# Eight-bit edge counts, four strips and counts dealt evenly to the steps, in a three-layer graph network on one core

## The chip, the core and the metric

The kernel runs on one core of one Trainium2 chip. The metric is device time in microseconds (us). The core has a matrix engine (TensorE, PE in the profile; its weight loads are PEld), a vector engine (VectorE, DVE), an activation engine (ScalarE, ACT), a general engine (GpSimd, POOL) and a queue engine (SyncE, SP). ACT, POOL and SP also issue transfers between DRAM and on-chip memory. Each engine works through its own instructions in program order.

## What is computed

A graph has N = 6250 nodes with 256 features and E = 200000 edges, sorted by their end node `dst`. End nodes follow a square law, so low nodes have by far the most edges: node 0 alone has some 2500, the last ones about 16. Start nodes `src` are random. Three graph convolutions come first, then a mixture-of-depths feed-forward layer:

```python
h = relu(gcn(layernorm(x), W1, b1)); h = relu(gcn(h, W2, b2)); x = x + gcn(h, W3, b3)
# gcn(h): msg = (h @ W)[src] * norm; segment_sum(msg, dst) + b
#         with one self-loop per node, norm = dinv[src] * dinv[dst]
weights = layernorm(x) @ wr + br          # the 3124 nodes of highest weight are chosen
y = (gelu(sel @ w1 + b1) @ w2 + b2) * w_sel
out = x_in_place_of_not_chosen + y_scattered_to_chosen   # residual on the layernormed x, added to x
```

## The kernel before

Nodes are cut into 49 tiles of 128. The first 31 tiles of end nodes (`DENSE`) are summed by **counts**: a matrix that holds, for each pair (start node, end node), how many edges join them. The sum over edges is then a matrix product of counts and node features. The other 18 tiles are summed by **gathers**: rows of start nodes are fetched by index, 128 edges at a time (a chunk; 359 chunks in 180 sets of two), and added to their end nodes with a one-hot matrix.

*One tile by counts.* A strip `[128, 49, 128]` in 16-bit floats holds a tile's counts for all 49 tiles of start nodes. It is used in seven pieces of seven start tiles. Each piece is one **step**: `piece_of` (L725) casts it to 32 bits, on ACT (L728) or, where `CASTS` says so, on VectorE (L730); `add_up` (L733) then does seven matmuls of 128x512 into the sum `c_pa` (L736). 512 columns are the features as a rounded part and a rest. `prepare` casts two steps ahead (`AHEAD`).

*Making counts (layer 0 only).* A window is 2, 3 or 4 neighbouring end nodes, with a fixed number of 128-edge slots, from an estimate of its edges. `one_hot` (L661, VectorE, L669) makes two one-hot tensors for K = 12 slots, `hot_w` for (start tile, end node in the window) and `hot_l` for the start node in its tile; each has two buffers. One count matmul (L689) per slot multiplies them into a window's place in a PSUM bank `ps_b` (two buffers). Windows fill a bank in threes (width 3), fives (width 2) or twos. `count_bank` (L678) makes a whole bank and evicts it to the strip on ACT (L705). `counted` (L714) checks the largest count of the one tile that could pass the exact range, adds the self-loops on VectorE (L722) and writes the strip to the DRAM tensor `counts` (L723), for layers 1 and 2.

*The order in layer 0.* All four compute engines follow an order written by hand. Tiles run from 30 down to 0, so the fullest comes last. Tile 30 is counted ahead of the loop. While a tile is summed, the next tile's banks are made, as planned in the table `place` (L830 to 834): the next tile's banks are divided evenly, by number of banks, over steps 0 to 4 of the seven, and between two banks comes a share of the step's seven sum matmuls (L902 to 906). There are two strips, used in turn. Count matmuls per step vary with the slots that windows have; for tile 0 they are 107, 71, 40, 46 and 42, for a tile of width 3 they are 9, 9, 9, 9 and 7.

*Gathers and the rest.* In each step a share of the sets is fetched by indirect transfers (L600, GpSimd), one-hot matrices are made (L609, VectorE), and in layers 1 and 2 the rows are split into two parts (L619 ACT, L624 VectorE). The matmuls are L632, with L637 for the self-loops. A finished tile goes through `total` (L527, L528), transposes (L287), the product with the next weights (L298) and a store (L545). Twenty columns of edge ends are fetched, coded and transposed into a `ps_b` bank (L795, `flip`) during the first layer.

*Layers 1 and 2* load each piece of counts from DRAM (`load`, L931: tile `whole`), cast it and sum as above. In layer 2, VectorE also does the residual and the norm (L549 to L576). The choice of nodes and the feed-forward layer follow.

Of the kernel before, what the change touches and what calls it, by code (L numbers as in the profile page):

```python
# [9 lines left out]
FP = mybir.dt.float32  # L10
FR = mybir.dt.float32r
F16 = mybir.dt.float16
BF = mybir.dt.bfloat16
I32 = mybir.dt.int32
U16 = mybir.dt.uint16
AF = mybir.ActivationFunctionType
AX = mybir.AxisListType
OP = mybir.AluOpType
# [3 lines left out]
P = 128  # L22
# [6 lines left out]
NT = (N + P - 1) // P  # L29
# [15 lines left out]


NOWHERE = 1 << 20
EXACT = 2048
RC = 200
RN = E // RC  # L50
K = 12
WMAX = 4
PIECE = 7
DENSE = 31
GB = 2
MSGS = [4, 7, 7]
LATE = [12, 6]
CASTS = [(0, 4), (0, 3), (3,)]
BANK = 512
# [7 lines left out]
def windows():  # L67

    banks = []
    for t in range(DENSE):  # L70
        n = P
# [16 lines left out]
BANKS = windows()  # L88
TILES_BY = list(range(DENSE))[::-1]

SOURCES = [(3, 2, 4, 1, 5, 6, 0), (0, 1, 2, 3, 5, 4, 6)]
SLOTS = [(a, w, c) for t in TILES_BY for bank in BANKS[t] for a, w, n in bank for c in range(n)]
WIDTH = [w for _, w, _ in SLOTS]
MOST = [max(n for bank in t for _, _, n in bank) for t in BANKS]
SD = ceil(len(SLOTS) / P)

CHUNKS = [(t, k, n) for t in range(DENSE, NT) for n in [chunks_of(t * P, t * P + P)] for k in range(n)]
# [10 lines left out]
def by_counts(  # L108
# [29 lines left out]


    rows = dram.tile([NP, 2 * D + 1], FP, name="c_rows")  # L140
    counts = dram.tile([DENSE, P, NT * P], F16, name="counts")

    sent = [dram.tile([NP, 2 * D if i == 0 else D], FR if i == 0 else FP, name=f"sent{i}") for i in range(3)]
    ends = {}
# [4 lines left out]
    b1p = build.enter_context(tc.tile_pool(name="b1p", bufs=1))  # L149
# [3 lines left out]
    f3p = hots.enter_context(tc.tile_pool(name="f3p", bufs=2))  # L153
# [57 lines left out]
    ident = keep.tile([P, P], FP, name="c_ident")  # L211
# [17 lines left out]
    ident_h = keep.tile([P, P], F16, name="c_ident_h")  # L229
    nc.vector.tensor_copy(ident_h, ident)  # L230
# [77 lines left out]
    for i, n in ((0, P), (1, NT)):  # L308
        made = f1p.tile([HP, HC, n], BF, name=f"hot_h{i}")
# [175 lines left out]
    later = {}  # L485
# [171 lines left out]
    ps_b = hots.enter_context(tc.tile_pool(name="ps_b", bufs=2, space=PSUM))  # L657
    later["g"] = hots.enter_context(tc.tile_pool(name="ps_g1", bufs=2, space=PSUM))
    hot = {}

    def one_hot(s):  # L661

        n = min(K, SD * P - s)
        assert {s // P, (s + n - 1) // P} <= columns_made
        wide = NT * max(WIDTH[s : s + K])
        made = []
        for up, cols, code, name in ((up_w, wide, codes[:, 0, s : s + n], "hot_w"), (up_l, P, codes[:, 1, s : s + n], "hot_l")):
            rows_k = b2p.tile([P, K // 2, up.shape[1], 2], F16, name=name)
            nc.vector.tensor_tensor(  # L669
                rows_k[:, : n // 2, :cols, :],  # L670
                up[:, None, :cols, :].to_broadcast([P, n // 2, cols, 2]),
                code.rearrange("p (k two) -> p k two", two=2)[:, :, None, :].to_broadcast([P, n // 2, cols, 2]),
                op=OP.is_equal,
            )
            made.append(rows_k)
        return made

    def count_bank(strip, t, bank, s):  # L678
        pb = ps_b.tile([P, BANK], FP, name="ps_b")
        at_c = 0  # L680
        for node, width, chunks in bank:
            for c in range(chunks):
                k = s % K
                if k == 0:
                    hot[s] = hot.pop(s, None) or one_hot(s)
                if k == K // 4 and s - k + K < len(WIDTH):
                    hot[s - k + K] = one_hot(s - k + K)
                row_w, row_l = hot[s - k]
                nc.tensor.matmul(  # L689
                    pb[:, at_c : at_c + NT * width],  # L690
                    row_l[:, k // 2, :, k % 2], row_w[:, k // 2, : NT * width, k % 2],
                    start=(c == 0), stop=(c == chunks - 1),
                )
                s += 1
                if k == K - 1:
                    hot.pop(s - K)
            at_c += NT * width

        at_c = 0
        i = 0  # L700
        while i < len(bank):
            node, width, _ = bank[i]
            n = sum(1 for w in bank[i:] if w[1] == width)
            d0 = node - t * P
            nc.scalar.activation(  # L705
                strip[:, :, d0 : d0 + n * width].rearrange("p h (a j) -> p h a j", j=width),
                pb[:, at_c : at_c + n * NT * width].rearrange("p (a h j) -> p h a j", a=n, j=width),
                AF.Copy,
            )
            at_c += n * NT * width  # L710
            i += n
        return s

    def counted(strip, t):  # L714
        if MOST[t] * P >= EXACT:
            top = small.tile([P, 1], FP, name="top")
            large = max(a - t * P + w for bank in BANKS[t] for a, w, n in bank if n * P >= EXACT)
            nc.vector.tensor_reduce(top, strip[:, :, :large], axis=AX.XY, op=OP.max)
            nc.vector.tensor_scalar(top, top, float(EXACT), None, op0=OP.is_ge)
            nc.vector.tensor_add(bad[:, 1:2], bad[:, 1:2], top)  # L720

        nc.vector.tensor_add(strip[:, t, :], strip[:, t, :], ident_h)  # L722
        nc.sync.dma_start(counts[t], strip.rearrange("p h d -> p (h d)"))  # L723

    def piece_of(layer, counts_7, i):  # L725
        piece = later["l3"].tile([P, PIECE, P], FR, name="piece")
# [17 lines left out]
    NS = NT // PIECE  # L744
    AHEAD = 2
# [79 lines left out]
    strips = {}  # L825
    pieces = {}
    s = 0
    order = [(t, i) for t in TILES_BY for i in range(NS)]

    place = {}  # L830
    for t, u in zip(TILES_BY, TILES_BY[1:]):
        m = len(BANKS[u])
        for i in range(NS - AHEAD):
            place[t, i] = BANKS[u][m * i // (NS - AHEAD) : m * (i + 1) // (NS - AHEAD)]

    now["due"] = pace(len(order) - 2 * NS, LATE[0]) + [SETS] * 2 * NS

# [26 lines left out]
    first_tile = TILES_BY[0]  # L864
# [2 lines left out]
    flip()  # L867
    next_step()
    send_x(1)
    strips[first_tile] = f3p.tile([P, NT, P], F16, name="strip", bufs=1)  # L870
# [13 lines left out]
    by_turn = [f3p, later["2"]]  # L884
    load_b(0, later["2"], nc.sync)
    load_w(1, later["2"], nc.sync)
    for n in range(AHEAD):
# [1 line left out]
    for n, (t, i) in enumerate(order):  # L889
        prepare(0, now, n, order, cast)  # L890

        flip()
        if taken and (taken[0][0] >= SD or (taken[0][0] - 2) * P <= s):
            next_column()
        if i == 0:
            pa = new_sums()
            u = TILES_BY[n // NS + 1] if n + NS < len(order) else None
            if u is not None:
                strips[u] = by_turn[(n // NS + 1) % 2].tile([P, NT, P], F16, name="strip", bufs=1)

        banks = place.get((t, i), [])
        m = max(1, len(banks))  # L902
        for k in range(m):
            if banks:
                s = count_bank(strips[u], u, banks[k], s)
            add_up(pa, pieces[n], i, range(PIECE * k // m, PIECE * (k + 1) // m))
        gathered(0, now, now["due"][n])
        if banks and i == NS - AHEAD - 1:
            counted(strips[u], u)
        pieces.pop(n)  # L910
        if i == NS - 1:
            onward(0, t, pa)
            strips.pop(t)
        next_step()
    finish()
    guard.close()
    firsts.close()
# [5 lines left out]
    l8p = lay.enter_context(tc.tile_pool(name="l8p", bufs=8))  # L923
# [5 lines left out]
    nc.sync.dma_start(wr_sb, wr.rearrange("d o -> o d").to_broadcast([P, D]))  # L929

    def load(t, i):  # L931
        whole = l8p.tile([P, PIECE, P], F16, name="whole")
        nc.sync.dma_start(
            whole.rearrange("p h d -> p (h d)"), counts[t][:, i * PIECE * P : (i + 1) * PIECE * P]
        )
        return whole

    with tc.manual_schedule(engines=ordered):
        for layer in (1, 2):
# [4 lines left out]
            order = [(t, i) for i in sources for t in range(2)]  # L944
# [74 lines left out]
    for i, (shift, n) in enumerate(DIGITS):  # L1019
# [7 lines left out]
            op=OP.is_ge,  # L1027
# [37 lines left out]
    place = places(kept, "place")  # L1065
# [14 lines left out]
    hot = ffn.tile([P, TC, NT], BF, name="hot")  # L1080
# [5 lines left out]
    for a in range(0, NT, PIECE):  # L1086
# [5 lines left out]
            op=OP.is_equal,  # L1092
        )
        for j in range(PIECE):
            t = a + j
# [19 lines left out]
    for g, n in enumerate(groups):  # L1115
        a = sum(groups[:g])
# [586 lines left out]
```

## Time and profile before

| What | Value |
|---|---|
| median of three runs | 2147.77 us (2144.26 to 2150.42) |
| profiled execution, its own time | 2141.61 us |
| its span, first to last instruction | 2139.8 us |
| busy PE / PEld | 1903.7 us (89%) / 1456.1 us (68%) |
| busy DVE / ACT / POOL | 1360.4 (64%) / 1162.1 (54%) / 1268.1 us (59%) |
| layer 0, first sum matmul to last tile's start | 144.0 to 847.0 us |
| count matmuls L689 | 2171, of them 1269 of 98 columns, 806 of 147, 96 of 196 |
| evictions L705 | 441, 247.8 us busy on ACT |
| loads `whole`<-`counts` | 434 of 224.0 KB |
| stores `counts`<-`strip` | 31 of 1568.0 KB |

The span leaves out 1.8 us around the first and the last instruction. A line of the page such as the two below names source line, engine, operation, what is written and read, the shape and the number, then busy us, mean ns of one, and the idle time of the engine ahead of them with what ended it. Here TensorE's largest group and its count matmuls:

```profile
L736 PE MATMUL c_pa<-hl,piece 128*128 128x512 f32 x4557 | 1257.5, 408 | 22.9 <-DVE hl L953 14.1
L689 PE MATMUL ps_b<-hot_w,hot_l 128*128 128x98 f16 (+2 forms) x2171 | 211.5, 224 | 60.5 <-DVE hot_l L669 49.5
```

Ends of matmuls are modelled and overlap their neighbours (408 ns is more than the distance between two), so distances between starts tell more than lengths do.

### The profile page before, as it was taken

How to read it: one execution, taken by the hardware profiler on the slowest of the kernel's cores; microseconds unless marked ns; L12 is line 12 of the kernel's file. 1: busy time of each engine (PE TensorE's matmuls, PEld its weight loads, DVE VectorE, ACT ScalarE, POOL GpSimd, SP SyncE). 2: the span in 40 equal slices, each digit the busy share in tenths (PEclk: the TensorE clock that was granted, in tenths of full speed). 3: DMA queues.
4: the chain of work that ended last, by engine and by line, in shares of the span. 5: the costliest groups of instructions: out<-in, count | busy, mean ns of one | idle time of the engine just before them, and what ended most of it. 6: DMA issues, size and time to landing. Idle time of an engine off the chain costs nothing.

```text
span 2139.8 us, 30448 instructions
## 1 busy us (share of the span) xinstructions
PE 1903.7 (89%) x9636; PEld 1456.1 (68%) x9636; DVE 1360.4 (64%) x3370; ACT 1162.1 (54%) x1986; POOL 1268.1 (59%) x1228
## 2 busy tenths in 40 slices
PE   4949999999999887799999999889999999928997
PEld 3726767777766666488888888667777777715665
DVE  7686565667677777555555555488888888862111
ACT  3676666656655533656555555576666665502111
POOL 5425777667766520477777777377777777602221
PEclk9969999999999999899999999999999999958999
DMA  8387888898977640877777777598888888612210
GB/s 211 93 295 227 248 256 267 246 269 231 274 217 205 197 145 36 290 235 224 215 215 210 215 213 214 170 285 261 255 256 255 255 255 251 205 58 62 60 48 17
DMA packets 229052, 435.60 MB, mean 204 GB/s; under 512 B 35358, under 2 KB 139092, under 8 KB 224881
## 3 DMA queue, kind: packets, MB, share of 16 engines
q0 software_dynamic: 92992, 205.70, 35.2%
q1 hardware_dynamic: 104357, 192.11, 28.0%
q10 hardware_dynamic: 31532, 35.75, 4.9%
q8 instruction: 78, 1.28, 0.2%
q14 instruction: 93, 0.76, 0.1%
HBM read 335.50 MB, written 99.61 MB: 203 GB/s over the span
## 4 chain that ended last, share of the span: by engine, by line
PE 60%; DVE 21%; DMA 8%; issue 4%; ACT 3%; POOL 3%; ACTq 0%; SPq 0%; POOLq 0%; DVEq 0%
PE c_pa L736 32%; PE ps_g L632 8%; PE c_po L1144 4%; PE c_ph L1136 4%; PE ps_b L689 4%; PE c_pt L298 4%; DVE hot_w L669 3%; DVE hot_l L669 3%; DVE half L624 2%; DMA msg<-sent,source 2%; DMA c_xt<-in_x 2%; DMA half<-sent,source 2%; POOL msg L600 2%; DVE pick_sel L609 1%; DVE c_z L528 1%
## 5 line engine op out<-in xcount | busy, mean ns | idle before, releaser
L736 PE MATMUL c_pa<-hl,piece 128*128 128x512 f32 x4557 | 1257.5, 408 | 22.9 <-DVE hl L953 14.1
L736 PEld LDWEIGHTS c_pa<-hl,piece 128*128 128x128 f32 x4557 | 828.1, 190 | 189.7 <-DVE hl L953 15.8
L600 POOL DMA_INDIRECT msg<-sent,source x718 | 733.3, 1021 | 346.6 <-issue 145.0
L600 POOL DMA_INDIRECT half<-sent,source x359 | 389.9, 1086 | 200.1 <-issue 75.6
L609 DVE TENSOR_TENSOR pick_sel<-up_h,local 128x256 fp32r<-128x256 f16 x540 | 227.8, 422 | 281.6 <-PE ps_g L632 280.4
L632 PE MATMUL ps_g<-half,pick_sel 128*128 128x512 f32 x1077 | 347.7, 401 | 40.1 <-DVE half L624 32.7
L619 ACT ACTIVATE half<-msg 128x512 fp32r<-128x512 f32 x360 | 225.4, 626 | 233.8 <-PE ps_g L632 157.3
L728 ACT ACTIVATE piece<-whole 128x896 fp32r<-128x896 f16 x341 | 320.2, 942 | 57.2 <-PE c_pa L736 31.2
L705 ACT ACTIVATE strip<-ps_b 128x441 f16<-128x441 f32 (+3 forms) x441 | 247.8, 570 | 175.5 <-PE ps_b L689 165.9
L624 DVE TENSOR_TENSOR half<-msg,half 128x512 fp32r<-128x512 f32 x360 | 248.7, 691 | 82.0 <-ACT half L619 80.4
L632 PEld LDWEIGHTS ps_g<-half,pick_sel 128*128 128x128 f32 x1077 | 200.2, 189 | 100.1 <-DVE half L624 49.0
L689 PE MATMUL ps_b<-hot_w,hot_l 128*128 128x98 f16 (+2 forms) x2171 | 211.5, 224 | 60.5 <-DVE hot_l L669 49.5
L689 PEld LDWEIGHTS <-hot_l 128*128 128x128 f16 x2171 | 133.4, 100 | 174.7 <-issue 104.0
L728 ACT ACTIVATE piece<-strip 128x896 fp32r<-128x896 f16 x159 | 151.2, 952 | 99.5 <-PE c_pa L736 94.3
L669 DVE TENSOR_TENSOR hot_w<-up_w,codes 128x1176 f16<-128x1176 f16 (+2 forms) x181 | 165.7, 915 | 41.8 <-PE ps_b L689 41.6
L669 DVE TENSOR_TENSOR hot_l<-up_l,codes 128x1536 f16<-128x1536 f16 x181 | 172.5, 953 | 0.0
L1140 ACT ACTIVATE ht<-c_ph,b_sb 128x512 f32<-128x512 f32 (+2 forms) x64 | 38.0, 594 | 186.4 <-PE c_ph L1136 186.2
L1152 POOL DMA_INDIRECT out<-o,pick x25 | 25.2, 1007 | 138.4 <-DVE o L1149 138.4
L1148 DVE TENSOR_TENSOR o<-c_po,b_sb 128x256 f32<-128x256 f32 x25 | 10.6, 425 | 149.2 <-PE c_po L1144 149.2
L298 PE MATMUL c_pt<-c_wg,c_zt 128*128 128x256 f32 x392 | 99.9, 380 | 0.5 <-ACT c_zt L293 0.5
L1136 PE MATMUL c_ph<-yt,w_sb 128*128 128x512 f32 (+2 forms) x256 | 89.4, 506 | 0.6 <-DVE yt L1131 0.6
L1144 PE MATMUL c_po<-w_sb,ht 128*128 128x256 f32 x400 | 88.0, 379 | 0.0
(218 smaller groups left out, 1532.0 us busy)
## 6 DMA issues: line engine op xcount, KB each, us to landing
whole<-counts SPq DMA_DIRECT2D x434, 224.0 KB
counts<-strip SPq DMA_DIRECT2D x31, 1568.0 KB
c_rows<-ys ACTq DMA_DIRECT2D x49, 256.5 KB
sent<-hl SPq DMA_DIRECT2D x7, 1792.0 KB
sent<-c_h ACTq DMA_DIRECT2D x98, 128.0 KB
message<-sent SPq DMA_DIRECT2D x98, 128.0 KB
msg<-sent,source POOLq DMA_INDIRECT x718
c_xt<-in_x SPq DMA_DIRECT2D x48, 128.0 KB
```

The source lines that it names most:

```text
L298: nc.tensor.matmul(pt[:, 1, :], zt[:, k, :], w_sb[:, k, :], start=(k == 0), stop=(k == KD - 1))
L600: nc.gpsimd.indirect_dma_start(out=out_j, out_offset=None, in_=sent[layer], in_offset=bass.IndirectOffsetOnAxis(ap=source[:, i : i + 1], a ...
L609: nc.vector.tensor_tensor(pick[:, :n], up_h[:, None, :].to_broadcast([P, n, P]), local[:, b * GB : b * GB + n, None].to_broadcast([P, n, P ...
L619: nc.scalar.activation(half[:, :n, 0, :], msg[:, :n], AF.Copy)
L624: nc.vector.tensor_sub(half[:, :n, 1, :], msg[:, :n], half[:, :n, 0, :].bitcast(FP))
L632: nc.tensor.matmul(open_sums[t], pick[:, j, :], half[:, j].rearrange("p two d -> p (two d)"), start=(k == 0), stop=False)
L669: nc.vector.tensor_tensor(rows_k[:, : n // 2, :cols, :], up[:, None, :cols, :].to_broadcast([P, n // 2, cols, 2]), code.rearrange("p (k tw ...
L689: nc.tensor.matmul(pb[:, at_c : at_c + NT * width], row_l[:, k // 2, :, k % 2], row_w[:, k // 2, : NT * width, k % 2], start=(c == 0), sto ...
L705: nc.scalar.activation(strip[:, :, d0 : d0 + n * width].rearrange("p h (a j) -> p h a j", j=width), pb[:, at_c : at_c + n * NT * width].re ...
L728: nc.scalar.activation(piece, counts_7, AF.Copy)
L736: nc.tensor.matmul(pa, piece[:, j, :], hl[:, q].rearrange("p two d -> p (two d)"), start=(i == sources[0] and j == 0), stop=(i == sources[ ...
L1136: nc.tensor.matmul(ph[:, : n * P], w1_sb[:, k, f * P : (f + 1) * P], yt[:, k, : n * P], start=(k == 0), stop=(k == KD - 1),)
```

## The change

1. Counts are held in eight-bit unsigned integers: the strips, the DRAM tensor `counts`, the identity that adds self-loops, and the loaded pieces `whole`.
2. An eviction whose windows have more than one slot (105 of the 441) also gives the sum of what it writes, per partition, into a column of `row_sums`. A new `all_counted` takes the largest of these sums once, at the end of layer 0, and flags a value of 255 or more. The check by tile in `counted` goes.
3. There are four strips in place of two, with half the bytes each, so the same memory. A tile's counts may be begun up to three tiles ahead.
4. `count_bank` is split into `count_window` and `evict`. The unit of the plan is a window, no longer a bank. A window costs its slots times (128 + columns); the plan goes through all steps and hands out windows at the lowest steady rate that meets every tile's deadline, two steps ahead of its first use. Within a step, single windows alternate with shares of the seven sum matmuls. A bank can stay open from one step to the next.

By this plan the count matmuls per step are 9 or 10 in the first four tiles (all seven steps), for instance 13, 13, 11, 0, 0, 14, 13 in the middle, and 18, 15, 18, 16, 18, 16, 16 in the 27th tile.

```diff
-EXACT = 2048
+EXACT = 255
+STRIPS = 4
-    counts = dram.tile([DENSE, P, NT * P], F16, name="counts")
+    counts = dram.tile([DENSE, P, NT * P], U8, name="counts")
-    def count_bank(strip, t, bank, s):
-        pb = ps_b.tile([P, BANK], FP, name="ps_b")
...
+    def count_bank(strip, t, bank, s):
+        for j in range(len(bank)):
+            s = count_window(bank, j, s)
+        evict(strip, t, bank)
+        return s
+    in_making = []
+    def count_window(bank, j, s):
+        if j == 0:
+            in_making.append(ps_b.tile([P, BANK], FP, name="ps_b"))
+        pb = in_making[0]
+        at_c = sum(NT * w for _, w, _ in bank[:j])
+        _, width, chunks = bank[j]
+        for c in range(chunks):
...
+    def evict(strip, t, bank):
+        pb = in_making.pop()
...
+            held = None
+            if max(w[2] for w in bank[i : i + n]) * P >= EXACT:
+                held = row_sums[:, len(summed_up) : len(summed_up) + 1]
+                summed_up.append(node)
             nc.scalar.activation(
...
                 AF.Copy,
+                accum_out=held,
             )
     def counted(strip, t):
-        if MOST[t] * P >= EXACT:
...
-        nc.vector.tensor_add(strip[:, t, :], strip[:, t, :], ident_h)
+        nc.vector.tensor_add(strip[:, t, :], strip[:, t, :], ident_8)
         nc.sync.dma_start(counts[t], strip.rearrange("p h d -> p (h d)"))
+    def all_counted():
+        top = small.tile([P, 1], FP, name="top")
+        nc.vector.tensor_reduce(top, row_sums[:, : len(summed_up)], axis=AX.X, op=OP.max)
+        nc.vector.tensor_scalar(bad[:, 1:2], top, float(EXACT), None, op0=OP.is_ge)
-    place = {}
-    for t, u in zip(TILES_BY, TILES_BY[1:]):
-        m = len(BANKS[u])
-        for i in range(NS - AHEAD):
-            place[t, i] = BANKS[u][m * i // (NS - AHEAD) : m * (i + 1) // (NS - AHEAD)]
+    todo = []
+    for k, u in enumerate(TILES_BY[1:], 1):
+        for bank in BANKS[u]:
+            for i, (_, w, c) in enumerate(bank):
+                todo.append((max(0, (k - STRIPS + 1) * NS - AHEAD), k * NS - AHEAD - 1, c * (P + NT * w), u, bank, i))
+    place = [[] for _ in order]
+    credit = 0
+    for n in range(len(order)):
+        rate = 0
+        ahead = -credit
+        for _, until, work_of, _, _, _ in todo:
+            ahead += work_of
+            rate = max(rate, ahead / (until - n + 1))
+        credit += rate
+        while todo and todo[0][0] <= n and todo[0][2] / 2 <= credit:
+            credit -= todo[0][2]
+            place[n].append(todo.pop(0)[3:])
+        credit = min(credit, todo[0][2] / 2) if todo else 0
-        banks = place.get((t, i), [])
-        m = max(1, len(banks))
+        made = place[n]
+        m = max(1, len(made))
         for k in range(m):
-            if banks:
-                s = count_bank(strips[u], u, banks[k], s)
+            if made:
+                u, bank, j = made[k]
+                if bank is BANKS[u][0] and j == 0:
+                    strips[u] = new_strip(u)
+                s = count_window(bank, j, s)
+                if j == len(bank) - 1:
+                    evict(strips[u], u, bank)
+                    if bank is BANKS[u][-1]:
+                        counted(strips[u], u)
             add_up(pa, pieces[n], i, range(PIECE * k // m, PIECE * (k + 1) // m))
-        whole = l8p.tile([P, PIECE, P], F16, name="whole")
+        whole = l8p.tile([P, PIECE, P], U8, name="whole")
```

More of the change, by code (lines that the diff above doesn't have):

```diff
@@ L15 @@
 U16 = mybir.dt.uint16
+U8 = mybir.dt.uint8
 AF = mybir.ActivationFunctionType
@@ L93 @@
 WIDTH = [w for _, w, _ in SLOTS]
-MOST = [max(n for bank in t for _, _, n in bank) for t in BANKS]
 SD = ceil(len(SLOTS) / P)
@@ L228, in by_counts @@
     nc.vector.tensor_scalar(last, diff_i, float(1 - P), None, op0=OP.is_equal)
-    ident_h = keep.tile([P, P], F16, name="c_ident_h")
-    nc.vector.tensor_copy(ident_h, ident)
+    ident_8 = keep.tile([P, P], U8, name="c_ident_8")
+    nc.vector.tensor_copy(ident_8, ident)
     ident_r = keep.tile([P, P], FR, name="c_ident_r")
@@ L678, in count_bank @@
     def count_bank(strip, t, bank, s):
-        pb = ps_b.tile([P, BANK], FP, name="ps_b")
[L680 to L697, printed above, removed]
+        for j in range(len(bank)):
[10 more added lines that the diff above has]
+        for c in range(chunks):
+            k = s % K
+            if k == 0:
+                hot[s] = hot.pop(s, None) or one_hot(s)
+            if k == K // 4 and s - k + K < len(WIDTH):
+                hot[s - k + K] = one_hot(s - k + K)
+            row_w, row_l = hot[s - k]
+            nc.tensor.matmul(
+                pb[:, at_c : at_c + NT * width],
+                row_l[:, k // 2, :, k % 2], row_w[:, k // 2, : NT * width, k % 2],
+                start=(c == 0), stop=(c == chunks - 1),
+            )
+            s += 1
+            if k == K - 1:
+                hot.pop(s - K)
+        return s
+    def evict(strip, t, bank):
+        pb = in_making.pop()
         at_c = 0
@@ L711, in count_bank @@
             i += n
-        return s
+    row_sums = b1p.tile([P, sum(len(t) + 1 for t in BANKS if max(w[2] for bank in t for w in bank) > 1)], FP, name="row_sums")
+    summed_up = []
     def counted(strip, t):
-        if MOST[t] * P >= EXACT:
[L716 to L722, printed above, removed]
+        nc.vector.tensor_add(strip[:, t, :], strip[:, t, :], ident_8)
         nc.sync.dma_start(counts[t], strip.rearrange("p h d -> p (h d)"))
+    def all_counted():
+        top = small.tile([P, 1], FP, name="top")
+        nc.vector.tensor_reduce(top, row_sums[:, : len(summed_up)], axis=AX.X, op=OP.max)
+        nc.vector.tensor_scalar(bad[:, 1:2], top, float(EXACT), None, op0=OP.is_ge)
     def piece_of(layer, counts_7, i):
@@ L828, in by_counts @@
     order = [(t, i) for t in TILES_BY for i in range(NS)]
-    place = {}
-    for t, u in zip(TILES_BY, TILES_BY[1:]):
-        m = len(BANKS[u])
-        for i in range(NS - AHEAD):
-            place[t, i] = BANKS[u][m * i // (NS - AHEAD) : m * (i + 1) // (NS - AHEAD)]
+    todo = []
[16 more added lines that the diff above has]
+        credit = min(credit, todo[0][2] / 2) if todo else 0
+    assert not todo
     now["due"] = pace(len(order) - 2 * NS, LATE[0]) + [SETS] * 2 * NS
@@ L869, in by_counts @@
     send_x(1)
-    strips[first_tile] = f3p.tile([P, NT, P], F16, name="strip", bufs=1)
+    strips[first_tile] = f3p.tile([P, NT, P], U8, name="strip0", bufs=1)
     next_column()
@@ L883, in by_counts, with new_strip @@
     later["2"] = firsts.enter_context(tc.tile_pool(name="firsts", bufs=2, side="right"))
-    by_turn = [f3p, later["2"]]
+    def new_strip(u):
+        k = TILES_BY.index(u) % STRIPS
+        return (later["2"] if k % 2 else f3p).tile([P, NT, P], U8, name=f"strip{k}", bufs=1)
     load_b(0, later["2"], nc.sync)
@@ L896, in by_counts @@
             pa = new_sums()
-            u = TILES_BY[n // NS + 1] if n + NS < len(order) else None
-            if u is not None:
-                strips[u] = by_turn[(n // NS + 1) % 2].tile([P, NT, P], F16, name="strip", bufs=1)
-        banks = place.get((t, i), [])
-        m = max(1, len(banks))
-        for k in range(m):
-            if banks:
-                s = count_bank(strips[u], u, banks[k], s)
+        made = place[n]
+        m = max(1, len(made))
+        for k in range(m):
+            if made:
[7 more added lines that the diff above has]
+                        counted(strips[u], u)
             add_up(pa, pieces[n], i, range(PIECE * k // m, PIECE * (k + 1) // m))
         gathered(0, now, now["due"][n])
-        if banks and i == NS - AHEAD - 1:
-            counted(strips[u], u)
         pieces.pop(n)
@@ L914, in by_counts @@
         next_step()
+    all_counted()
     finish()
```

## The prediction

> **What bounds the kernel now.** I read the busy time by stretch first. The page's shares mix stages that have different limits, so I cut at the first matmul of layer 0's sums (144 us), inside that layer, at its last tile (847 us) and at the layers. The columns are: length, then busy us (and instructions) of PE, PEld, DVE, ACT and POOL, then PE clock, DMA share, GB/s.
>
> ```profile
> 144.00:410.00 266.00, 256.17 (x1467) 184.81 (x1468) 162.40 (x290) 182.58 (x309) 179.49 (x168) 0.99 0.83 253
> 410.00:607.00 197.00, 188.00 (x1258) 140.12 (x1257) 135.65 (x251) 119.89 (x199) 139.91 (x133) 1.00 0.87 254
> 607.00:734.00 127.00, 117.09 (x786) 87.34 (x786) 96.54 (x155) 70.90 (x119) 80.47 (x71) 1.00 0.71 209
> 734.00:847.00 113.00, 88.50 (x798) 67.87 (x795) 90.45 (x141) 42.45 (x69) 23.80 (x21) 0.92 0.33 100
> ...
> 960.00:1360.00 400.00, 400.00 (x1790) 327.99 (x1789) 225.88 (x433) 230.27 (x355) 300.19 (x296) 1.00 0.74 214
> ...
> 1420.00:1860.00 440.00, 410.74 (x1735) 325.17 (x1735) 368.61 (x1180) 275.85 (x427) 336.70 (x329) 0.99 0.86 253
> ```
>
> Layer 0 is TensorE's until about 734 us (95 to 96% busy). Then come three tiles in which TensorE falls to 78% and VectorE rises to 80%. Layer 1 is TensorE alone, without a gap. In layer 2 TensorE has gaps.
>
> The waits of 734 to 847 us name who is late there. The columns are the sum in us, the times, and the longest:
>
> ```profile
> PEld L689 <- DVE hot_l L669: 29.8, 33, 2.5
> PE ps_b L689 <- DVE hot_l L669: 24.5, 33, 2.1
> ```
>
> VectorE makes the one-hot rows (L669), 0.77 + 0.95 = 1.72 us for each 12 count matmuls. The counts of tile 0 need 306 matmuls, and the plan puts them all into five steps.
>
> Then I read the timeline of TensorE in a layer-0 tile without a wait, for the price of a count matmul between sums (start, length, what):
>
> ```profile
> 541.90 0.41 PE L689 MATMUL ps_b<-hot_w,hot_l 128*128 128x98 f16 x5
> 542.13 0.72 PE L736 MATMUL c_pa<-hl,piece 128*128 128x512 f32 x2
> 542.68 0.40 PE L689 MATMUL ps_b<-hot_w,hot_l 128*128 128x98 f16 x5
> 542.90 0.71 PE L736 MATMUL c_pa<-hl,piece 128*128 128x512 f32 x2
> 543.57 0.39 PE L689 MATMUL ps_b<-hot_w,hot_l 128*128 128x98 f16 x5
> ```
>
> Read starts, since the ends are modelled. Five counts take 542.13 - 541.90 = 0.23 us, 0.045 each. The two sum matmuls behind them take 542.68 - 542.13 = 0.55 us. In a run of their own a sum matmul follows its neighbour after 0.231 us (layer 1: seven and two gather matmuls from 1096.89 to 1099.06, less 0.08). So the pair costs 0.55 - 0.46 = 0.09 us too much. Start by start, the first sum matmul behind counts takes 0.314 instead of 0.231, and the last one ahead of counts 0.238. That holds for one count (13 cases) as for five (69 cases). **A group of counts between sums costs 0.090 us, however small it is.**
>
> With these pitches I add up layer 0 from 144.0 to 847.0 us (30 tiles, 703.1 us) in the program's order: 1470 sums x 0.231 = 339.6; 377 gather matmuls x 0.231 = 87.1; 130 transposes x 0.107 = 13.9; 94 products x 0.432 = 40.6; 1269 counts x 0.0445, 803 x 0.058 and 64 x 0.076 = 108.1; 425 groups and 15 other changes 38.9. Sum 628.2 us. Tiles without a wait agree within 0.1 us, so 703.1 - 628.2 = 74.9 us are waits: 5.2 in the first tile, 19.2 in the next 21 (transfers of gathered rows and one-hot rows), 50.5 in the last eight.
>
> In layer 2 the reader is to look at GpSimd:
>
> ```profile
> 1380.13 1.10 POOL L600 DMA_INDIRECT msg<-sent,source  x1 [26.26 <-DMA sent<-c_h]
> 1381.55 1.03 POOL L600 DMA_INDIRECT msg<-sent,source  x1 [0.31 <-issue]
> 1382.88 0.95 POOL L600 DMA_INDIRECT msg<-sent,source  x1 [0.30 <-issue]
> ```
>
> It issues 359 gathers from 1380.1 to 1862.2 us, one each 1.34 us, with the 0.30 us of issue between them and practically nothing else. TensorE needs only 14.3 us for a tile of this layer (tiles without gaps), GpSimd 11.6 x 1.34 = 15.5; the tiles take 15.6 on average. Layer 2 is bound by the issue of gathers, although DMA is 86% busy and the waits name VectorE.
>
> **The change, part by part.** All against the profiled execution, 2141.6 us.
>
> *Dealing by window.* Before, whole banks of 3 or 5 windows were made, three or so in each of five steps. Now single windows go to all seven steps, and each is followed by a seventh or more of a step's seven sum matmuls. In the order of the two built programs the groups between sums grow from 425 to 1111, mostly of one or two matmuls; the count matmuls stay 2171. 686 x 0.090 and a few other changes = +62.7 us. This lies on the path, as TensorE is the bound in nearly all of layer 0: 690.9 us without any wait. Here the Trainium skill speaks for the change: TensorE: Matmul & The Clock Gate, in the table of specifications at its head, says that TensorE pulls weight loads ahead of matmuls in flight. By that rule the small groups would cost nothing and layer 0 would need 628 us. The row speaks against it: the weights of the count at 542.68 us start with the count itself, 0.23 us after the sum matmul ahead of it, not during it. I take the row.
>
> *Evening out with four strips.* The counts of the last tiles are begun up to three tiles ahead. Matmuls beside tiles 27 to 29 fall from 133, 213, 233 to 125, 112, 81, and the last eight tiles have 825 instead of 994. Their TensorE sum is 195.5 us (before 189.7, taken 240.3). VectorE there loses 169/12 = 14 sets x 1.72 = 24 us of 204. It stays at 179 of 195, and the fullest tiles (117 matmuls: 17 us of rows and 8 of other work in 26) have no slack. The rows have two buffers, so VectorE can't get far ahead: I take 18 us of waits for the 50.5, between 8 (spread evenly, every peak is absorbed) and 32 (as before in tiles with VectorE over 90%). In the first 22 tiles TensorE needs 495.4 instead of 438.4. Their waits shrink, because VectorE and the transfers have more time: 4 for the first tile and 11 for the rest, of 24.4. In that 11 is a new wait. A bank now stays open over the start of a step, where the transposes of an edge column (L795) take the other of two ps_b buffers; the next bank stands behind the open bank's eviction, and the sums stand behind it on TensorE: 18 times, 0 to 0.6 us. Sum for layer 0: 690.9 + 4 + 11 + 18 = 724, against 703: **+21 us** (-2 to +36).
>
> *Eight bits on chip.* Evictions (441 on ACT, 581 ns median) and ACT's casts (952 ns) have the same elements. ACT is 69% busy or less in layer 0, and early tiles with 22 banks instead of 15 give it 19 of 24 us. The sum output on 105 of the evictions has no row here. The nearest is VectorE's own accumulator read, 82 ns: 9 us of ACT in tiles where it has 10 us free each, so 0, and up to 5 if it were three times that. VectorE's work is where a width could count:
>
> ```profile
> L722 DVE TENSOR_TENSOR strip<-strip,c_ident_h x31: 217/226/282, 139.9 to 843.8; 128x128 f16<-128x128 f16 x31
> L730 DVE CAST piece<-strip x58: 614/622/735, 143.2 to 776.9; 128x896 fp32r<-128x896 f16 x58
> ```
>
> VectorE: DVE Perf Modes, under what auto-detection checks, asks for 16-bit tensors on all sides for the packed two-element mode, but only for SBUF on both sides for the two-port mode. By it the add loses its mode: 67 ns x 31 = 2 us. The cast keeps its 622 ns. Were the cast at one element a cycle, it would be some 470 ns longer: 58 in layer 0 (into a full VectorE at the end: up to +8 us) and 31 in layer 2, where GpSimd covers most (up to +7). I take 0 and keep the 15 for the range.
>
> *Bytes.* Strips go out at 784 instead of 1568 KB; 434 loads in layers 1 and 2 bring 112 instead of 224 KB. By packet times (1792 bytes 74 ns, 1024 bytes 46) the loads' third of DMA time falls to about 0.19. In layer 1 it is hidden by TensorE, in layer 2 by GpSimd's issue. Does a freer DMA make the issue faster? In layer 1 issues under a busy DMA are longer, in layer 2 not, so 0 to -7 us. At the layers' starts some loads come sooner: -3 in all, 0 to -10.
>
> *The check.* One reduction of 248 ns and two small ones at the end of layer 0 are replaced by two: 0. The fallback isn't taken: a bank of ten nodes holds at most some 8000 edges, 62 in a row of sums, far from 255.
>
> Total: +21 - 3 = +18, so 2160 us for a profiled execution. The median shown, 2147.8, is 6.2 above the profiled one: **2166 us**.
>
> **Rivals.**
> - *The small groups are cheap* (faster). If alternation lets the weights through, the price falls in the 686 new groups, for instance to half: 62.7 becomes 31, the total -13, 2135 us. It turns from loss to gain at 44/686 = 0.064 us per group. For it: the skill's rule, and no row with a single sum matmul between two groups. Against it: 13 groups of a single count that pay the full price.
> - *All waits go* (no change). If only the first tile's 4 us and some 11 more stay, layer 0 takes 706 and the time is 2148. For it: tiles at 85% VectorE had no wait. Against it: two row buffers and tiles at 95%.
> - *DMA was layer 2's bound.* If the halved loads bring each issue to its shortest, 1.25 us, 359 x 0.09 = 32 us go: 2134. Against it: 0.3 us gaps whatever the DMA share.
> - *Eight bits slow VectorE and ACT*: +15 to +20 more, 2183.
>
> **How the numbers follow.** The price of groups with most waits gone: 0.66, centred on 2166; with slow 8-bit work 0.05; all waits gone, about even, 0.16; cheap groups or a layer 2 freed by DMA, 0.13. A measurement of this kernel can tell 0.3% from no change, 6.4 us. So slower 0.71, same 0.16, faster 0.13. The range goes from 2137 (nearly all waits gone, with the relief by DMA) to 2185 (slow 8-bit work).
>
> **What would show it.** Right: count groups of one or two in TensorE's timeline, the sum matmul behind each with a pitch of 0.31 us; early tiles at 23 to 25 us where they took 19 to 23; the last eight tiles about 213 us in all; layer 0's last tile starting at about 868 us, not 847; GpSimd in layer 2 still at 1.34 us per gather with half the load bytes; casts at 622 ns. It is wrong if the pitch in fine alternation is near 0.23, if waits for L669 vanish, or if layer 2 shortens by over 10 us.

## The result, and the profile after

The changed kernel takes 2166.74 us in the median of five runs (2162.45 to 2168.23); the kernel before takes 2147.77 us beside it (2143.52 to 2153.97). The ratio is 1.0088, 95% interval 1.007 to 1.0106: slower, by 19 us. The predicted time was 2166.

The profiled execution of the changed kernel took 2168.23 us, its span is 2166.4 us; before, the span was 2139.8. So the two profiles differ by 26.6 us and the medians by 19.0, because the profiled execution of before lay 6.2 us below its median and that of the changed kernel 1.5 above. Differences between traces below are to be read against the 26.6.

The stretches of the changed kernel, in the same cut as before (first sum matmul of layer 0, inside it, its last tile, layers 1 and 2; columns as in the prediction):

```profile
145.00:410.00 265.00, 256.33 (x1428) 167.36 (x1429) 167.02 (x292) 178.69 (x311) 163.48 (x152) 0.99 0.71 199
410.00:658.00 248.00, 240.20 (x1469) 164.43 (x1467) 161.25 (x285) 140.92 (x256) 159.39 (x149) 0.99 0.72 194
658.00:755.00 97.00, 90.82 (x597) 61.08 (x594) 75.70 (x125) 51.98 (x132) 59.52 (x52) 0.98 0.62 166
755.00:870.80 115.80, 108.05 (x814) 76.22 (x815) 84.19 (x133) 49.25 (x103) 43.20 (x39) 1.00 0.44 119
980.00:1380.00 400.00, 400.00 (x1783) 326.79 (x1783) 225.24 (x431) 230.33 (x355) 300.52 (x298) 1.00 0.58 164
1440.00:1880.00 440.00, 409.37 (x1725) 321.20 (x1724) 365.82 (x1172) 273.65 (x424) 337.95 (x326) 1.00 0.73 202
```

TensorE is now 93% busy in the last 116 us of layer 0, where it was 78% busy. The dip is gone, and layer 0 is longer all the same. From the first sum matmul of layer 0 to the start of its last tile it takes 725.8 us instead of 703.1: the first 22 tiles 513.0 instead of 462.8, the last eight 212.8 instead of 240.3. The DMA share falls from 0.74 to 0.58 in layer 1 and from 0.86 to 0.73 in layer 2, and neither layer is shorter: they end 24.0 us late where they began 23.8 us late. The rest of the kernel adds 2.6 us.

Why a fuller TensorE takes longer is seen in its timeline (start, length, what) in the 18th tile of layer 0:

```profile
540.14 0.27 PE L700 MATMUL ps_b<-hot_w,hot_l 128*128 128x98 f16 x2
540.23 0.47 PE L757 MATMUL c_pa<-hl,piece 128*128 128x512 f32 x1
540.54 0.26 PE L700 MATMUL ps_b<-hot_w,hot_l 128*128 128x98 f16 x2
540.62 0.47 PE L757 MATMUL c_pa<-hl,piece 128*128 128x512 f32 x1
540.94 0.26 PE L700 MATMUL ps_b<-hot_w,hot_l 128*128 128x98 f16 x2
541.02 0.48 PE L757 MATMUL c_pa<-hl,piece 128*128 128x512 f32 x1
```

From start to start, a sum matmul and its two counts take 540.54 - 540.14 = 0.40 us. Without a price they would take 0.231 + 2 x 0.0445 = 0.32. Between two groups a single sum matmul takes 0.32 us instead of 0.231 (540.23 to 540.54 is 0.31). The median is 0.321 us over all 900 such sums of layer 0; the trace of before had one. TensorE counts as busy all the time, so no list of waits shows this.

The most frequent group of one is a single count of 147 columns (269 cases). Here it is in the second tile:

```profile
172.75 0.24 PE L700 MATMUL ps_b<-hot_w,hot_l 128*128 128x147 f16 x1
172.79 0.48 PE L757 MATMUL c_pa<-hl,piece 128*128 128x512 f32 x1
173.11 0.24 PE L700 MATMUL ps_b<-hot_w,hot_l 128*128 128x147 f16 x1
```

The pair takes 173.11 - 172.75 = 0.36 us, and without a price it would be 0.231 + 0.058 = 0.29. The sum again takes 0.32, but the count only 0.04 (median 0.040), where its share of a full group was 0.058. So this group costs 0.07 us, not 0.09.

What is left of the waits for one-hot rows in the last tiles (us in total, times, longest):

```profile
PEld L700 <- DVE hot_l L670: 11.8, 12, 2.4
...
PE ps_b L700 <- DVE hot_l L670: 9.2, 9, 2.2
```

Before, the two lines were 29.8 and 24.5.

### The profile page after: what moved, and what is told of

The parts are those of the page before. It is cut to its first block, busy times and chain, and to the rows that moved or that the text cites. A ratio compares the mean times of both kernels' runs of the same rounds, so it can differ in the third digit from the quotient of the medians.

```text
span 2166.4 us, 30530 instructions
## 1 busy us (share of the span) xinstructions
PE 1952.2 (90%) x9636; PEld 1445.2 (67%) x9636; DVE 1362.4 (63%) x3369; ACT 1166.6 (54%) x2091; POOL 1270.0 (59%) x1228
## 4 chain that ended last, share of the span: by engine, by line
PE 65%; DVE 20%; DMA 6%; ACT 4%; issue 3%; POOL 1%; ACTq 0%; SPq 0%; POOLq 0%; DVEq 0%
PE c_pa L757 35%; PE ps_g L633 9%; PE ps_b L700 6%; PE c_ph L1178 4%; PE c_po L1186 4%; PE c_pt L299 4%; DVE half L625 3%; DMA msg<-sent,source 2%; DMA message<-sent 2%; DVE pick_sel L610 1%; DVE hot_l L670 1%; DVE hot_w L670 1%; DVE c_z L529 1%; DVE piece L751 1%; DVE c_z L528 1%
## 5 line engine op out<-in xcount | busy, mean ns | idle before, releaser
L757 PE MATMUL c_pa<-hl,piece 128*128 128x512 f32 x4557 | 1356.4, 421 | 21.8 <-DVE hl L995 14.2
L757 PEld LDWEIGHTS c_pa<-hl,piece 128*128 128x128 f32 x4557 | 855.9, 190 | 182.2 <-issue 20.6
L700 PE MATMUL ps_b<-hot_w,hot_l 128*128 128x98 f16 (+2 forms) x2171 | 324.1, 225 | 45.5 <-DVE hot_l L670 29.3
L724 ACT ACTIVATE strip<-ps_b 128x441 uint8<-128x441 f32 (+3 forms) x441 | 248.1, 572 | 214.9 <-PE ps_b L700 211.4
L749 ACT ACTIVATE piece<-whole 128x896 fp32r<-128x896 uint8 x341 | 319.6, 941 | 50.9 <-PE c_pa L757 34.8
L625 DVE TENSOR_TENSOR half<-msg,half 128x512 fp32r<-128x512 f32 x360 | 248.2, 689 | 87.7 <-ACT half L620 87.1
L700 PEld LDWEIGHTS <-hot_l 128*128 128x128 f16 x2171 | 145.8, 99 | 229.7 <-issue 138.8
L749 ACT ACTIVATE piece<-strip 128x896 fp32r<-128x896 uint8 x159 | 150.9, 951 | 74.2 <-PE c_pa L757 66.7
```

What stands on the lines that cost most here:

```text
L625: nc.vector.tensor_sub(half[:, :n, 1, :], msg[:, :n], half[:, :n, 0, :].bitcast(FP))
L700: nc.tensor.matmul(pb[:, at_c : at_c + NT * width], row_l[:, k // 2, :, k % 2], row_w[:, k // 2, : NT * width, k % 2], start=(c == 0), sto ...
L724: nc.scalar.activation(strip[:, :, d0 : d0 + n * width].rearrange("p h (a j) -> p h a j", j=width), pb[:, at_c : at_c + n * NT * width].re ...
L749: nc.scalar.activation(piece, counts_7, AF.Copy)
L757: nc.tensor.matmul(pa, piece[:, j, :], hl[:, q].rearrange("p two d -> p (two d)"), start=(i == sources[0] and j == 0), stop=(i == sources[ ...
```

## The experiments

They ran on other chips than the result, in three series (e, f, g), in which the kernel before takes 2413, 2385 and 2383 us instead of 2148. The ratio of each is to the kernel before of the same series. The extra time lies mostly in layers 1 and 2 (some 90 us each); layer 0 has more waits there too.

Most of the reading is of layer 0. The TensorE sum adds up, for each trace, the median distance from a matmul to the next, by the kinds of the two and of the one ahead; what is left of the measured time is mostly waits. (By the pitches of the prediction, the sum of the rows with small groups is some 12 us higher, because a count in a small group is shorter.) The columns on lateness add up, in us, by how much counts start late, where it is over 0.06 us against that median: first counts of a batch of one-hot rows, then other first counts of a bank. For the chip of the result the same reading is in the two upper rows.

| Kernel | groups | TensorE sum | layer 0, us | left | late batches | late banks | ratio to before |
|---|---|---|---|---|---|---|---|
| before, on the chip of the result | 425 | 626 | 703.1 | 77 | 54 | 8 | |
| changed, on the chip of the result | 1111 | 679.5 | 725.8 | 46 | 30 | 13 | 1.0088 |
| e1: eight bits only, whole banks, old plan | 425 | 629 | 744.7 | 116 | 60 | 41 | 1.0003 |
| f2, g1: whole banks dealt evenly | 425 | 630 | 742.0, 746.6 | 112, 117 | 67, 68 | 31, 34 | 1.0005, 1.0013 |
| e2, g4: single windows alternate, old plan | 1156 | 682 | 772.3, 761.4 | 91, 80 | 35, 35 | 36, 29 | 1.0068, 1.0084 |
| f1, g3: the changed kernel | 1111 | 679 | 752.7, 749.3 | 73, 71 | 32, 32 | 33, 32 | 1.0031, 1.0058 |
| e4: at most three groups in a step | 517 | 638 | 762.8 | 125 | 50 | 51 | 1.0017 |
| e3: at most two groups in a step | 350 | 626 | 762.7 | 137 | 55 | 67 | 1.0068 |
| g2: as g1, one-hot rows made further ahead | 425 | 630 | 721.6 | 92 | 29 | 44 | 0.9877 |

Each trace is one execution, and the same kernel differs by 11 us in layer 0 between e2 and g4. Differences of this size between series say nothing. The kernel before was not traced there; e1, which has its plan, stands for it.

**e1, the eight bits alone.** From the changed kernel, with the old plan of whole banks in five of seven steps:

```diff
-    todo = [...]   # windows, all steps, by work
+    for k, u in enumerate(TILES_BY[1:]):
+        m = len(BANKS[u])
+        for i in range(NS - AHEAD):
+            place[k * NS + i] = [(u, bank) for bank in BANKS[u][m * i // (NS - AHEAD) : m * (i + 1) // (NS - AHEAD)]]
```

> Eight bits, sums on evictions and four strips of half size, but the old plan: whole banks of the next tile in steps 0 to 4, 425 groups of counts. Price theory (the loss is the 686 extra groups at 0.09 us each, 62 us, less the waits that even dealing removes): layer 0 like before, 703 us less about 5 us of waits for transfers in early tiles, layers 1 and 2 within 3 us: ratio to before 0.996 to 1.000, about 2143 us. Rival (eight bits or the sums on evictions are slow on ACT or VectorE): above 2155 us. Rival (the halved transfers free layer 2): below 2130 us, with layer 2 at least 10 us shorter.

Measured: 1.0003 (0.9973 to 1.0033). Eight bits, the sums on evictions and a sixth less traffic together are worth nothing that can be measured, to within 0.3%. What the change loses beyond that is in the plan.

**e2 and g4, the alternation alone.** From the kernel before, in 16 bits:

```diff
-        for node, width, chunks in bank:
+        for w, (node, width, chunks) in enumerate(bank):
+            if between and w:
+                between()        # a share of the step's seven sums
```

> The kernel before, 16 bits and the old plan by step, but within a step the sum matmuls are put between single windows, so 1156 groups of counts in place of 425, all else the same. Price theory: 694 us of TensorE work in layer 0 in place of 628, +66 us; the last tiles, where VectorE is the bound, and waits elsewhere take up some 20 of these, so layer 0 takes about 749 us in place of 703 and the time is 2194 us (2180 to 2210). Rival (weights of small groups are loaded ahead, the groups are free and the loss comes from banks that stay open and from evictions): no change, 2148 us within 7.

> The kernel before with the sums put between its single windows (1156 groups instead of 425, sixteen bits, two strips, whole banks in five of seven steps as before), as in e2_alternate_only. If before takes about 2150 us here: price of 731 more groups 66 us, less up to 40 us of waits that the mixing takes away, so 26 to 66 us, 1.012 to 1.031. If before takes about 2390 us: 1.003 to 1.010, as in e2. Rival (groups are free): 1.000 or below.

Measured: 1.0068 (1.0032 to 1.0104) and 1.0084 (1.0049 to 1.0119). e2 misses its range, which was for a chip like that of the result; g4 is within its own. The sign is that of the price, the size about half of it or less: layer 0 is 28 and 17 us longer than e1's, where the added groups cost 53. The table shows where the rest went: the same alternation takes 25 to 36 us of waits away, and late batches fall from 60 to 35. The pitch of a single sum between groups is 0.32 us here as well, so the price isn't smaller; it is partly paid out of waits.

**e3 and e4, fewer groups by force.** From the changed kernel, each step's windows in at most two or three groups:

```diff
-        m = max(1, len(made))
+        m = max(1, min(2, len(made)))        # e4: 3
         for k in range(m):
-            if made:
-                u, bank, j = made[k]
+            for u, bank, j in made[len(made) * k // m : len(made) * (k + 1) // m]:
```

> The kernel after, with the same windows in the same steps, but each step's windows in at most two groups between shares of the sum matmuls: 350 groups in place of 1111. Price theory: 622 us of TensorE work in layer 0 in place of 691, and if the waits stay at 35 us, 657 us in place of 726: about 2098 us (2085 to 2120, more waits for evictions being the open term, since two and more banks now follow each other with two buffers). Rival (groups are free): 2167 us or more.

> As the one with at most two groups, but three: 517 groups, 637 us of TensorE work in layer 0. Price theory: 672 us with waits of 35, about 2113 us (2100 to 2125), 15 us above the one with two groups, less what evictions make that one wait. Rival (groups are free): 2167 us.

Measured: 1.0068 (1.0043 to 1.0092) and 1.0017 (0.9981 to 1.0052). Both miss by far. The price is saved in the sum (626 and 638 us), but layer 0 is not shorter than the changed kernel's on these chips. The largest part of the answer is the open term of the expectation, the evictions: late banks are 67 and 51 us where the changed kernel has 32 to 33. Late batches rise too, from 32 to 55 and 50. TensorE's waits in e3's first 22 tiles, and then in those of the changed kernel on such a chip:

```profile
PE ps_b L700 <- ACT strip L724: 30.8, 45, 2.4
...
PE ps_b L700 <- DVE hot_l L670: 16.9, 14, 3.2
```

```profile
PE ps_b L700 <- ACT strip L724: 15.2, 18, 3.7
...
PE ps_b L700 <- DVE hot_l L670: 7.5, 7, 2.4
```

And one place of it in e3's timeline (in brackets the idle time ahead and what ended it):

```profile
414.62 0.24 PE L700 MATMUL ps_b<-hot_w,hot_l 128*128 128x147 f16 x1
415.09 0.36 PE L700 MATMUL ps_b<-hot_w,hot_l 128*128 128x147 f16 x3 [0.24 <-ACT strip L724]
416.41 0.23 PE L700 MATMUL ps_b<-hot_w,hot_l 128*128 128x147 f16 x1 [0.96 <-ACT strip L724]
416.44 0.94 PE L757 MATMUL c_pa<-hl,piece 128*128 128x512 f32 x3
```

Five counts lie across three banks, with nothing between them; there are two `ps_b` buffers, and the eviction takes 0.58 us on ACT. TensorE stands idle where it would have done sums.

**f1 and g3, the changed kernel itself** on these chips.

> The changed kernel itself, unedited, on the same chip as the other three of this call. Price theory: 1.0088 of before (interval 1.007 to 1.011), and layer 0 longer than before's by about 23 us. If the chip is again one whose kernel before takes some 2400 us, the difference should stay near 20 us, so 1.005 to 1.011. Rival (the price of groups is a matter of one chip): below 1.003.

> The changed kernel unedited, on the chip of this call. 1.007 to 1.011 of before if before takes about 2150 us here; 1.001 to 1.005 if it takes about 2390, as in f1_after_again.

Measured: 1.0031 (1.0012 to 1.0051) and 1.0058 (1.0032 to 1.0084). Slower in both, by 11 us of the medians instead of 19. f1 is below its range of 1.005 to 1.011, and g3 just above its range. Layer 0 is 5 to 8 us longer than e1's in another series, not 23. This fits the waits: with the old plan more of them lie there to be taken away (116 us left in e1, 77 in the kernel before on the chip of the result).

**f2 and g1, evening out alone.** From the changed kernel, whole banks dealt evenly by work over all steps, up to three tiles ahead:

```diff
-            for i, (_, w, c) in enumerate(bank):
-                todo.append((..., c * (P + NT * w), u, bank, i))
+            cost = sum(c * (P + NT * w) for _, w, c in bank)
+            todo.append((..., cost, u, bank))
...
-                s = count_window(bank, j, s)
+                s = count_bank(strips[u], u, bank, s)
```

> The changed kernel, eight bits, four strips and even dealing kept, with whole banks dealt instead of single windows: 425 groups of counts instead of 1111, each bank's counts in one piece with sums behind it, so that two banks never follow each other without sums between, as they did with two and three groups a step. Price theory: TensorE's sum for layer 0 is 629 us instead of 691; waits at the start of a bank about 15, at the start of a batch of twelve counts 18 to 25; layer 0 about 665 to 675 us against 703 before and 726 after. Run: 0.981 to 0.987 of before (2108 to 2120 us where before takes 2148). Rival (mixing single counts with sums is what takes the waits away, and the price of groups is only what is paid for that): the 40 us of waits come back, layer 0 is about 700 and the run is 0.997 to 1.003.

> Whole banks dealt evenly, eight bits, four strips, as in f2_banks_even, on another chip if one is given. On the chip of f2 layer 0 was 742 us against 753 for the changed kernel, with 62 us of waits at the start of batches of twelve counts and 29 at the start of banks. Price theory with those waits: layer 0 shorter than the changed kernel's by 10 to 40 us; 0.985 to 0.998 of before on a chip where before takes about 2150 us, 0.998 to 1.003 where it takes about 2390. Rival (single counts mixed with sums are needed to keep the waits away): not faster than the changed kernel.

Measured: 1.0005 (0.9984 to 1.0027) and 1.0013 (0.9988 to 1.0037). The price is gone (425 groups), and my theory falls with its gain of 13 to 19 per thousand: the waits come back in full, 112 and 117 us against e1's 116. Evening out moves them. The last eight tiles take 223 and 225 us instead of e1's 249, the first 22 take 519 and 522 instead of 496. Of f2's rival the range and the cause hold: what keeps the late batches away in the changed kernel is the mixing of single counts with sums. But whole banks are 10 us faster than the changed kernel by the medians in both series, which g1's rival denies. g1's ratio is in its range, and its layer 0 is only 3 us below g3's, not 10 to 40.

**g2, one-hot rows further ahead.** As g1, with batches of 8 counts instead of 12, three buffers instead of two, and each batch made two ahead:

```diff
-K = 12
+K = 8
-    b2p = hots.enter_context(tc.tile_pool(name="b2p", bufs=2))
+    b2p = hots.enter_context(tc.tile_pool(name="b2p", bufs=3))
-            if k == K // 4 and s - k + K < len(WIDTH):
-                hot[s - k + K] = one_hot(s - k + K)
+            if k == K // 4 and s - k + 2 * K < len(WIDTH):
+                hot[s - k + 2 * K] = one_hot(s - k + 2 * K)
```

> As g1, with batches of eight counts instead of twelve, three buffers for each operand instead of two, and a batch made two batches ahead instead of one. If the waits at the start of a batch come from VectorE making it too late (about one batch ahead), most of the 62 us go and layer 0 is 25 to 45 us shorter than g1's; the run is 1 to 2% below g1. Rival (VectorE has no time left in those stretches, so that a longer lead only moves the wait): layer 0 within 8 us of g1's. [...]

Measured: 0.9877 (0.9843 to 0.9911) of before, and 2352.4 us against 2394.3 for the changed kernel on the same chip, 42 us less by the medians. Against g1 it is 31 us less, and layer 0 is 25 us shorter, the lower end of what was expected. TensorE's waits for one-hot rows in layer 0 of g1, then of g2:

```profile
PEld L700 <- DVE hot_l L670: 57.4, 49, 3.7
PE ps_b L700 <- DVE hot_l L670: 47.9, 45, 3.6
```

```profile
PEld L702 <- DVE hot_l L670: 17.9, 29, 2.5
PE ps_b L702 <- DVE hot_l L670: 12.3, 20, 2.3
```

Two thirds of these waits or more are gone, though VectorE makes the same rows: it had the time, and had been asked too late. In exchange the waits for evictions (`ps_b` on ACT, L726) rise from 13.9 to 28.0 us. The edit changes batch size, buffers and lead together, so it does not tell which of them counts. This version beats both kernels on this chip. On the chip of the result it was not run.

**f3 and f4, what holds layer 2.** Half the bytes of each gather, or half the gathers (both leave out part of layer 2's data):

```diff
+            if layer == 2:       # f3, f4: the two edits are apart
+                out_j, in_j = out_j[:, : D // 2], in_j.rearrange("n (c d) -> (n c) d", c=2)
...
-        for j in range(min(GB, len(CHUNKS) - b * GB)):
+        for j in range(min(GB if layer < 2 else 1, len(CHUNKS) - b * GB)):
```

> The changed kernel, in which layer 2's gathers fetch half a row each (512 bytes instead of 1024, from another place of the table, and used twice), as many gathers as before. Part of layer 2's data is thereby left out. Issue theory (layer 2 waits for GpSimd's gathers, one per 1.34 us, whatever their bytes): layer 2 stays within 5 us of the changed kernel's 476 us. Rival (layer 2 waits for bytes to arrive): TensorE's 34 us of waits for halved messages go by 15 us or more.

> The changed kernel, in which layer 2 issues one gather for each two chunks, and uses it for both: 180 gathers instead of 359, the same work on every other engine. Half of layer 2's gathered rows are thereby left out. Issue theory: TensorE's 34 us of waits for halved messages go for the most part, layer 2 takes 440 to 456 us instead of 476. Rival (VectorE's other work in layer 2, busy 395 of 476 us, or the transfers of whole strips set the pace): layer 2 stays within 8 us of 476.

Measured: layer 2, from its 50th sum matmul on, takes 567.8 us in the changed kernel on this chip, 573.6 with half the bytes, 462.8 with half the gathers (runs: 1.003 and 0.9608 of before). This stretch in f1, f3 and f4:

```profile
1560.00:2127.80 567.80, 473.91 (x1847) 363.11 (x1846) 397.22 (x1256) 298.39 (x472) 348.67 (x345) 0.93 0.61 168
```

```profile
1551.40:2125.00 573.60, 470.00 (x1847) 358.30 (x1846) 398.01 (x1256) 297.53 (x471) 348.70 (x345) 0.95 0.48 128
```

```profile
1555.00:2017.80 462.80, 435.14 (x1847) 343.06 (x1847) 393.10 (x1257) 298.98 (x474) 175.96 (x173) 1.00 0.56 158
```

In f3 the DMA share falls by a fifth, and no engine's busy time moves by more than 5 us. In f4 GpSimd has half the work and the layer is 105 us shorter, three times what I expected: on this chip a gather comes each 1.60 us on average, not each 1.35, so there is more to win. Gathers hold layer 2 there by their number, not their bytes.

## Why the prediction was right, and where it was not

*The price of a group* (step "dealing by window") was right in kind and too high in size. A single sum between groups takes 0.32 us, as forecast, in 900 cases of a kind that the trace of before had once. But "however small it is" does not hold. The 13 single counts in the trace of before all had 98 columns; a single count of 147 takes 0.040 us and not 0.058, and two take 0.106 and not 0.116. All counts together take 97 us in layer 0, where the prediction had 108. So TensorE's sum grows by 53 us (626 to 679.5), not by 62.7: some 0.078 us for each of the 686 new groups. The rule that weight loads are pulled ahead of matmuls in flight (Trainium skill, TensorE: Matmul & The Clock Gate, table of specifications) does not bring the price to nothing in the groups seen here: the pitch of 0.32 us stands against it. The rival of cheap groups is out.

*The waits* were the term that came out too low. Layer 0's 725.8 us less 679.5 leaves 46 us, predicted 33. In the last eight tiles it is 19 (predicted 18, before 50). In the first 22 it is some 27, as before, where the prediction had them fall to 15. Late starts of gather matmuls fell there from 8.3 to 0.4 us, as forecast. But late banks rose from 9.0 to 15.5 (with those that also begin a batch), and late batches stayed at 12 to 13.

*Layer 0 in all* is 22.8 us longer (predicted 21), and its last tile starts at 870.8 us (predicted 868). That this fits so well is in part luck: the price was 9 us too high and the waits 13 us too low. The five tiles behind the first take 23.4, 23.7, 25.8, 22.8 and 23.1 us (predicted 23 to 25). The new wait at the start of a step was there and small: 1.8 us at the transposes and 1.6 us behind the codes, of 0 to 11.

*The reason for the waits' going was wrong in part.* The step "evening out with four strips" says that VectorE and the transfers have more time because counts are begun earlier. f2 and g1 have that, and their late batches are 67 and 68 us against e1's 60. e2 and g4 have the mixing alone and come to 35; both together, in f1 and g3, come to 32. So the mixing does it. By the pitches: six groups of two counts and a sum take 6 x 0.40 = 2.4 us for a batch of twelve, longer than the 1.72 us in which VectorE makes one; a bank of ten counts with three or four sums behind takes 10 x 0.0445 + 3.5 x 0.231 + 0.09 = 1.34 us, which is 1.6 us for twelve, shorter than 1.72. The arithmetic is an argument; g2, where an earlier batch takes late batches to 29 us without mixing, supports it. So the price and the relief are two sides of one edit, 53 us paid for some 31 us of waits on the chip of the result.

*Eight bits on chip* cost nothing, as taken. The widths behaved as the rule of the Trainium skill, VectorE: DVE Perf Modes (what auto-detection checks), says: the strip's add rose from 226 to 291 ns, 65 ns for predicted 67, and the casts stayed at 620 ns (622 before).

```profile
L738 DVE TENSOR_TENSOR strip<-strip,c_ident x31: 277/291/293, 140.9 to 867.9; 128x128 uint8<-128x128 uint8 x31
...
L751 DVE CAST piece<-strip x58: 612/620/807, 144.2 to 831.4; 128x896 fp32r<-128x896 uint8 x58
```

The term for the sum output was mis-sized. It shows as an instruction of its own behind 105 evictions:

```profile
L724 ACT ACTIVATION_READ_ACCUMULATOR strip<-ps_b x105: 178/194/258, 601.0 to 867.7; 128x1 f32 x105
```

That is 20.3 us of ACT, not 9. ACT has it to spare: 49 of 116 us busy in the last stretch, and e1, which has the same reads, is no slower.

*Bytes* gave 0, not -3. The step's reason (layer 2 held by the issue of gathers) is borne out by f3 and f4 on their chip; on the chip of the result neither was run. There the gathers of layer 2 come each 1.353 us (1.344 before), though 896-byte packets take 41 ns where 1792 took 74. The small gains at the layers' starts did not appear.

*The sum.* On the profile's scale I had +18; it is +26.6: 1.8 from layer 0, 3 from bytes that gave nothing, 2.6 from the feed-forward part and 1.0 from the start, which I had at nothing. I added 6.2 us as the distance from a profiled execution to the median; that distance was -1.5 for the changed kernel. The closeness of 2166.7 to 2166 owes something to these two errors having opposite signs, besides those inside layer 0. The mechanism, a loss through the price of groups in layer 0, owes nothing to luck.

Open: what makes layers 1 and 2 longer on the chips of the experiments. Most distances between gathers are the same there (median 1.25 us in layer 2 on both), but in f1 32 of layer 2's are over 2.5 us, 4.1 on average, where the chip of the result has two. Such pauses stand in layer 1 too: GpSimd's longest group of waits there, for message buffers, is 74.7 us in 28 times, released by VectorE's L625. What starts a pause is not shown.

## What to carry to other kernels

A matmul of another kind set between large ones can cost more by its place than by its length, and a busy engine hides that: count the changes of kind and read the pitch from start to start. Before spreading small work out to take waits away, ask what the waiting engine's supplier lacks: here it lacked notice, not time, and an earlier batch took most of these waits without the price. And when a price is read from small cases, look at what they are: here all single counts had the narrow shape. When pieces of work share a two-buffer pool, putting them side by side can turn the eviction into a wait.

## What the runs showed of the hardware

- A group of 16-bit matmuls between 32-bit ones of 512 columns costs 0.07 to 0.09 us: the large matmul behind it has a pitch of 0.314 us, or 0.32 between two groups, instead of 0.231, on all chips used. The least, 0.07, is for a single matmul of 147 columns or two of 196.
- A sum output on an activation adds an instruction of 194 ns on ACT behind it.
- On one chip halving a gather's bytes did not shorten layer 2 (573.6 us for 567.8), and halving their number did (462.8). GpSimd's shortest distance between two gathers was 1.24 to 1.25 us on every chip.
- The same program took 11 to 12% longer on other chips, in f1 some 180 of 231 us in layers 1 and 2, at a mean granted clock of 0.92 to 0.94 instead of 0.96.
